# Layer 0 by dense scores and layers 1 to 3 with TensorE in program order, in place of layer 0 on neighbour lists

## The chip, the core and the metric

The kernel runs on one core of a Trainium2 chip. The time is the device time of one execution in microseconds, the median of several runs. The core's engines work side by side and wait for each other through semaphores: PE (TensorE, matrix products; PEld is its weight load), DVE (VectorE), ACT (ScalarE), POOL (GpSimd) and SP (SyncE, which only issues transfers). SBUF is the on-chip memory, PSUM the memory into which TensorE writes.

## The reference

Four graph attention layers over 3327 nodes with 256 features, all on one adjacency matrix `adj` (3327 x 3327, about 33 neighbours a node, itself included). After each layer comes x = layernorm(x + layer(x)). All is float32.

```python
# layer 0: additive scores, a leaky relu inside the sum over the 256 channels
g = leaky_relu(g_src[:, None, :] + g_tgt[None, :, :], 0.2)
score = where(adj != 0, einsum('ijc,c->ij', g, a_w), -inf)
x = layernorm(x + softmax(score) @ g_tgt)
# layer 1: e = leaky_relu(s1[:, None] + s2[None, :]); softmax over neighbours; @ Wh
# layer 2: the same without the leaky relu
# layer 3: two passes of a layer with four heads of 64 channels, each followed by elu
```

Layer 0 is the expensive one if it is done densely: its relu stands inside the channel sum, so a score needs 256 relus for each pair of nodes. Layers 1 to 3 have scores of the form relu(s_i + t_j), which are made from two vectors.

## The kernel before

Nodes lie in 26 row tiles of 128 (the last has 127), held as `h[0]` to `h[25]`.

**Layer 0 (`sparse0`).** Two projections of every tile are made (lines 228 and 233); the target rows go to a table in HBM. Then, tile by tile, `neighbours` (lines 244 to 297) makes a list of up to 56 neighbour numbers of each row on DVE from the adjacency, and casts the transposed adjacency to bf16 for the later layers (`turned` on ACT, line 277, stored to `at_d`). For each list place one gather on POOL's queue fetches 128 table rows (line 310); DVE makes the scores (lines 319 to 329), ACT the softmax weights (line 337), and each weight becomes a diagonal matrix on ACT (line 343) by which TensorE adds up the gathered rows (line 344). `lost` counts neighbours that found no place in a list. If there are any, a branch at the program's end runs `dense0` and `layers` over again; with these inputs it isn't taken.

**`dense0`** (lines 357 to 522) stands in the program for that branch. For a row tile it makes three passes over the columns (1024, 1024 and 1279 wide). A row's relu over all targets is one instruction on `[128 channels, width]`, the row's source value being a scalar for each channel; five of eight go to DVE, three to ACT (`turn % 8`). TensorE then sums over the channels with the attention vector: a 32-column window of zeros with the vector in one column puts the result into the row's own PSUM partition. Four rows, one in each group of 32 partitions, form a set that is multiplied span by span (512 wide). The relus have eight buffers, which is two sets. `finish0` makes softmax and the weighted sum in pieces that are dealt out among the next tile's sets.

**Layers 1 to 3 (`layers`).** Target columns are taken in four blocks of 7, 7, 6 and 6 tiles. Within a block a step is one tile j of 128 source nodes. `weigh` makes a step's weights for the block's columns: a relu on ACT (line 633), then plus one and times the adjacency on DVE (line 637), in a tile `e` that has six buffers. `one_head` (layers 1 and 2) multiplies them with the features into one PSUM bank for each tile of the block (line 730). `many_heads` (layer 3, run twice) makes eight products of 64 columns a step (line 769: four heads, two column halves, two heads sharing a bank), and eight sums of weights of 32 columns (line 776: four heads share a bank); the loop takes a half's four products and then its four sums. At a block's end come reciprocal, spread over the channels by a small product, and elu (lines 788 to 801). `pending` holds generators that prepare the next layer, taken on by one piece a step (`work_off`); `work_until` empties it where something is needed.

**Order.** The framework's scheduler orders the instructions of each engine ahead of time by priorities and expected times; the program order is only its starting point. In a layer-3 step it let the products of 64 columns alternate with the sums of 32.

Of the kernel before, what the change touches and what calls it, by code (L numbers as in the profile page):

```python
# [17 lines left out]
P = 128  # L18
# [5 lines left out]

KMAX = 56
CHUNK = 64
CHUNKS = 52
PIECES = 4

ROW = 260  # L30
# [3 lines left out]
def gat_stack(  # L34
# [55 lines left out]
    table_d = dram.tile([nt * P, ROW], F32, name="table_d")  # L90
# [30 lines left out]
    def attend(it, prob, proj, pool, psum, acc, col, width, copies):  # L121
# [45 lines left out]
    def residual_norm(dst, acc, total, skip, pn):  # L167

        inv = small.tile([P, 1], F32, tag="inv", name="inv")
        nc.vector.reciprocal(inv[:pn], total[:pn])  # L170
        y = work.tile([P, dim], F32, tag="y", name="y")
        nc.vector.scalar_tensor_tensor(
            y[:pn], acc, inv[:pn], skip, op0=ALU.mult, op1=ALU.add
        )
        norm(dst, y[:pn], pn)
# [7 lines left out]


    def sparse0(lost):
        with ExitStack() as s0:
            const0 = s0.enter_context(tc.tile_pool(name="s_const", bufs=1))
            io0 = s0.enter_context(tc.tile_pool(name="s_io", bufs=2))
            gath = s0.enter_context(tc.tile_pool(name="gath", bufs=11))
            ps0 = s0.enter_context(tc.tile_pool(name="s_ps", bufs=2, space=PSUM))  # L190

            w_src = const0.tile([P, kc, dim], F32, name="w_src0")
            nc.sync.dma_start(w_src, w_src_t.rearrange("(c p) f -> p c f", p=P))
            w_tgt = const0.tile([P, kc, dim + 1], F32, name="w_tgt0")
            nc.sync.dma_start(w_tgt[:, :, :dim], w_tgt_t.rearrange("(c p) f -> p c f", p=P))
            a_row = load_row(a_w, "src")
            bs_row = load_row(b_src, "dst")
            bt_row = load_row(b_tgt, "bias")
            dots(w_tgt[:, :, dim : dim + 1], w_tgt, a_row, 1)
            nc.vector.tensor_scalar_mul(  # L200
                w_tgt[:, :, dim], w_tgt[:, :, dim], SLOPE / (1.0 - SLOPE)
            )
            n_pad = CHUNK * CHUNKS
            rev = const0.tile([P, n_pad], F32, name="rev")
            for lo in range(0, n_pad, n_pad // PIECES):
                rev_i = io0.tile([P, n_pad // PIECES], I32, tag="adj_i", name="rev_i")
                nc.gpsimd.iota(
                    rev_i, pattern=[[-1, n_pad // PIECES]], base=n - lo, channel_multiplier=0
                )
                nc.vector.tensor_copy(rev[:, lo : lo + n_pad // PIECES], rev_i)  # L210

            x_t_p = x_t.rearrange("(c p) n -> p c n", p=P)
            for it in range(nt):
                pn = rows_of(it)
                xt = io0.tile([P, kc, P], F32, tag="xt", name="xt")
                nc.sync.dma_start(xt[:, :, :pn], x_t_p[:, :, it * P : it * P + pn])
                row = io0.tile([P, ROW], F32, tag="row", name="row")
                nc.vector.memset(row[:, dim + 1 :], 0.0)  # L220
                if pn < P:
                    nc.vector.memset(row[:, :dim], 0.0)
                    nc.vector.memset(row[:, dim : dim + 1], -BIG)
                    nc.vector.memset(h[it], 0.0)
                pt = ps0.tile([P, BANK], F32, tag="pt", name="pt")
                pss = ps0.tile([P, BANK], F32, tag="ps", name="pss")
                for k in range(kc):
                    nc.tensor.matmul(
                        pt[:pn, : dim + 1], xt[:, k, :pn], w_tgt[:, k, :],
                        start=(k == 0), stop=(k == kc - 1),  # L230
                    )
                for k in range(kc):
                    nc.tensor.matmul(
                        pss[:pn, :dim], xt[:, k, :pn], w_src[:, k, :],
                        start=(k == 0), stop=(k == kc - 1),
                    )
                nc.vector.tensor_add(row[:pn, :dim], pt[:pn, :dim], bt_row[:pn])
                nc.scalar.copy(row[:pn, dim : dim + 1], pt[:pn, dim : dim + 1])
                nc.vector.scalar_tensor_tensor(
                    h[it][:pn], pss[:pn, :dim], -1.0, bs_row[:pn],  # L240
                    op0=ALU.mult, op1=ALU.subtract,
                )
                nc.sync.dma_start(table_d[it * P : (it + 1) * P, :], row)

            def neighbours(it):

                pn = rows_of(it)
                cand = io0.tile([P, CHUNKS, 8], F32, tag="cand", name="cand")
                sums = io0.tile([P, PIECES + 1], F32, tag="sums", name="sums")
                per = CHUNKS // PIECES  # L250
                for s in range(PIECES):
                    lo = s * per * CHUNK
                    hi = min(n, lo + per * CHUNK)
                    adj_i = io0.tile([P, per * CHUNK], I32, tag="adj_i", name="adj_i")
                    nc.sync.dma_start(
                        adj_i[:pn, : hi - lo], adj[it * P : it * P + pn, lo:hi]
                    )
                    v = io0.tile([P, per * CHUNK], F32, tag="num", name="num")
                    if pn < P:
                        nc.vector.memset(v, 0.0)  # L260
                        nc.vector.memset(sums[:, s : s + 1], 0.0)
                    elif hi - lo < per * CHUNK:
                        nc.vector.memset(v[:, hi - lo :], 0.0)
                    nc.vector.scalar_tensor_tensor(
                        v[:pn, : hi - lo], adj_i[:pn, : hi - lo], 0.0, rev[:pn, lo:hi],
                        op0=ALU.not_equal, op1=ALU.mult, accum_out=sums[:pn, s : s + 1],
                    )
                    for c in range(per):
                        nc.vector.max(  # L269
                            cand[:, s * per + c, :], v[:, c * CHUNK : (c + 1) * CHUNK]  # L270
                        )
                    turned_i = io0.tile([P, per * CHUNK], I32, tag="turned_i", name="turned_i")
                    nc.sync.dma_start(
                        turned_i[:pn, : hi - lo], adj_t[it * P : it * P + pn, lo:hi]
                    )
                    turned = io0.tile([P, per * CHUNK], BF16, tag="turned", name="turned")
                    nc.scalar.copy(turned[:pn, : hi - lo], turned_i[:pn, : hi - lo])  # L277
                    nc.sync.dma_start(at_d[it * P : it * P + pn, lo:hi], turned[:pn, : hi - lo])
                found = io0.tile([P, KMAX], F32, tag="found", name="found")
                for r in range(0, KMAX, 8):  # L280
                    nc.vector.max(found[:, r : r + 8], cand)
                    if r + 8 < KMAX:
                        nc.vector.match_replace(
                            out=cand, in_to_replace=found[:, r : r + 8], in_values=cand,
                            imm_value=0.0,
                        )
                nc.vector.tensor_reduce(
                    sums[:, PIECES : PIECES + 1], found, axis=AX.X, op=ALU.add, negate=True
                )
                nc.vector.tensor_reduce(  # L290
                    lost[:, it : it + 1], sums, axis=AX.X, op=ALU.add
                )
                index = io0.tile([P, KMAX], mybir.dt.uint32, tag="index", name="index")
                nc.vector.tensor_scalar(
                    index, found, -1.0, float(n), op0=ALU.mult, op1=ALU.add
                )
                return index

            GROUP = 8
            for it in range(nt):  # L300
                pn = rows_of(it)
                index = neighbours(it)
                xr = io0.tile([P, dim], F32, tag="xr", name="xr")
                nc.sync.dma_start(xr[:pn], x[it * P : it * P + pn, :])
                sc = io0.tile([P, KMAX], F32, tag="scores", name="scores")
                gs = []
                for k0 in range(0, KMAX, GROUP):
                    g = gath.tile([P, GROUP, ROW], F32, tag="g", name="g")
# [214 lines left out]

# [433 lines left out]
```

## Time and profile before

| | |
|---|---|
| median of 3 runs | 5398.13 us (5394.32 to 5399.33) |
| the profiled execution | 5394.32 us, span 5392.5 us |
| mean granted TensorE clock | 0.801 |
| PE busy | 3236.2 us, 60% of the span |
| DVE busy | 2670.5 us, 50% |
| ACT busy | 1733.2 us, 32% |
| POOL busy | 1560.0 us, 29% |

The profile is of one execution. A group of instructions is named by line, engine, operation, output and inputs, with its number (x), its busy time in us, the mean duration of one in ns, and the idle time of the engine in front of them with what ended it. A float32 product leaves two records of TensorE. The stretches used below are cut where the last instruction of layer 0 ends (2829 us), where layer 2's products begin (3213), and at the begin and end of the two layer-3 passes (3545, 4461, 5364).

### The profile page before, as it was taken

To read this page: it belongs to the slowest core of one execution; us is meant where nothing else is said; L and a number is where in the kernel's file an instruction comes from. 1 tells how busy PE (TensorE), PEld (TensorE's weight loads), DVE (VectorE), ACT (ScalarE), POOL (GpSimd) and SP (SyncE) were. 2 spreads that over 40 slices of the span, in tenths; PEclk is the share of its full clock that TensorE was granted. 3 is DMA by queue.
4 is the path that set the end of the run, shared out by engine and by line. 5 is a ranking of instruction groups with operands and counts; after the bars stand their busy time and mean duration, and the time that the engine had idled before them with its cause. 6 is when DMAs were issued, how large, how long until landed. Compare 5 with 4: busy or idle time off the path is not lost.

```text
span 5392.5 us, 45944 instructions
## 1 busy us (share of the span) xinstructions
PE 3236.2 (60%) x14134; PEld 1624.5 (30%) x14134; DVE 2670.5 (50%) x7569; ACT 1733.2 (32%) x3049; POOL 1560.0 (29%) x1504
## 2 busy tenths in 40 slices
PE   4232121231231231232149999999999999999998
PEld 3131121221231131131137887642222222222222
DVE  6455255555555555555543541134445554455555
ACT  1243111221221121131133431134445554444544
POOL 2655266556556556556540000000000000000000
PEclk8666566666566676565669999999999999999999
DMA  8888344544545544544532222211000010010110
GB/s 254 180 215 209 68 98 93 87 95 93 88 94 93 88 94 94 84 97 94 83 62 57 63 63 75 59 40 28 21 25 23 25 29 23 26 30 27 31 31 23
DMA packets 199258, 413.05 MB, mean 77 GB/s; under 512 B 40830, under 2 KB 125800, under 8 KB 199008
## 3 DMA queue, kind: packets, MB, share of 16 engines
q0 software_dynamic: 69888, 193.92, 21.5%
q1 hardware_dynamic: 129120, 216.12, 13.8%
q8 instruction: 118, 1.93, 0.1%
q14 instruction: 132, 1.08, 0.1%
HBM read 380.89 MB, written 29.01 MB: 76 GB/s over the span
## 4 chain that ended last, share of the span: by engine, by line
PE 44%; DVE 2%; DMA 1%; POOL 1%; issue 1%; ACT 1%; POOLq 0%; SPq 0%; DVEq 0%; ACTq 0%
PE acc L769 17%; PE acc L776 13%; PE acc L730 8%; PE misc L617 2%; PE misc L578 2%; POOL g L310 1%; DMA at<-at_d 1%; PE acc L344 1%; PE misc L658 0%; DMA g<-table_d,index 0%; ACT e L633 0%; DVE stats L700 0%; DVE h L743 0%; POOL rstds L704 0%; DVE e L637 0%
## 5 line engine op out<-in xcount | busy, mean ns | idle before, releaser
L344 PE MATMUL acc<-g,diag 128*128 128x256 f32 x2912 | 697.2, 404 | 2039.3 <-ACT diag L343 2036.2
L310 POOL DMA_INDIRECT g<-table_d,index x1456 | 1520.8, 1044 | 1230.8 <-PE acc L344 708.6
L637 DVE SCALAR_TENSOR_TENSOR e<-e,at 128x896 f32<-128x896 f32 (+2 forms) x936 | 927.0, 1024 | 1012.5 <-ACT e L633 952.3
L633 ACT ACTIVATE e<-rate,minus_one,feat 128x896 f32<-128x896 f32 (+2 forms) x936 | 946.3, 1071 | 973.6 <-PE acc L776 849.5
L344 PEld LDWEIGHTS acc<-g,diag 128*128 128x128 f32 x2912 | 591.7, 205 | 2144.8 <-ACT diag L343 2056.3
L769 PE MATMUL acc<-e,feat 128*64 128x384 f32 (+4 forms) x3328 | 1007.2, 535 | 9.5 <-DVE e L637 9.2
L319 DVE TENSOR_TENSOR y<-g,h 128x1024 f32<-128x1024 f32 x364 | 444.6, 1223 | 926.4 <-DMA g<-table_d,index 926.4
L776 PE MATMUL acc<-e,feat 128*32 128x384 f32 (+4 forms) x3328 | 783.9, 525 | 0.0
L704 POOL TENSOR_TENSOR rstds<-rstds,minus_half 128x7 f32<-128x7 f32 (+1 forms) x12 | 20.1, 1676 | 2528.3 <-DVE rstds L703 2453.1
L343 ACT ACTIVATE diag<-ident,w 128x128 f32<-128x128 f32 x1456 | 544.4, 398 | 59.7 <-PE acc L344 29.7
L337 ACT ACTIVATE w<-scores,top 128x56 f32<-128x56 f32 x26 | 8.9, 341 | 1671.1 <-DVE top L334 1671.1
L325 DVE SCALAR_TENSOR_TENSOR y<-y,src 128x256 f32<-128x256 f32 x1456 | 525.7, 419 | 0.1
L769 PEld LDWEIGHTS acc<-e,feat 128*64 128x64 f32 (+1 forms) x3328 | 250.1, 135 | 712.9 <-issue 527.1
L730 PE MATMUL acc<-feat,e 128*128 128x257 f32 (+2 forms) x1352 | 306.7, 380 | 0.0
L776 PEld LDWEIGHTS acc<-e,feat 128*32 128x32 f32 (+1 forms) x3328 | 123.3, 107 | 577.9 <-issue 572.7
L730 PEld LDWEIGHTS acc<-feat,e 128*128 128x128 f32 (+2 forms) x1352 | 253.8, 190 | 35.7 <-issue 1.6
L730 PE MATMUL acc<-feat,at 128*128 128x257 bf16 (+2 forms) x2028 | 247.8, 279 | 16.0 <-DMA at<-at_d 16.0
L730 PEld LDWEIGHTS <-at 128*128 128x128 bf16 (+2 forms) x2028 | 202.7, 101 | 61.2 <-DMA at<-at_d 17.1
L277 ACT CAST turned<-turned_i 128x832 bf16<-128x832 int32 (+1 forms) x104 | 91.9, 883 | 395.9 <-DMA turned_i<-in_adj_t_dram 395.7
L269 DVE MAX8 cand<-num 128x8 f32<-128x64 f32 x1352 | 217.8, 212 | 1.8 <-DMA table_d<-row 1.4
L163 DVE TENSOR_SCALAR h<-y,mv,rstd 128x256 f32<-128x256 f32 (+1 forms) x26 | 12.0, 460 | 288.0 <-POOL rstd L162 288.0
L325 DVE DVE_READ_ACCUMULATOR y<-y,src 128x1 f32 x1456 | 118.8, 82 | 0.0
(108 smaller groups left out, 1490.5 us busy)
## 6 DMA issues: line engine op xcount, KB each, us to landing
at<-at_d SPq DMA_DIRECT2D x200, 224.0 KB
turned_i<-in_adj_t_dram SPq DMA_DIRECT2D x75, 416.0 KB
adj_i<-in_adj_dram SPq DMA_DIRECT2D x75, 416.0 KB
g<-table_d,index POOLq DMA_INDIRECT x1456, 3.6
at<-at_d SPq DMA_DIRECT2D x100, 192.0 KB
at<-at_d SPq DMA_DIRECT2D x100, 191.8 KB
at_d<-turned SPq DMA_DIRECT2D x75, 208.0 KB
adj_i<-in_adj_dram SPq DMA_DIRECT2D x25, 415.5 KB
```

Of the source, the lines that this page charges most:

```text
L269: nc.vector.max(cand[:, s * per + c, :], v[:, c * CHUNK : (c + 1) * CHUNK])
L310: nc.gpsimd.indirect_dma_start(out=g[:, s, :], out_offset=None, in_=table_d[:, :], in_offset=bass.IndirectOffsetOnAxis(ap=index[:, k0 + s ...
L319: nc.vector.tensor_tensor(y, g[:, part : part + 4, :dim], h[it][:, None, :].to_broadcast([P, 4, dim]), op=ALU.max,)
L325: nc.vector.scalar_tensor_tensor(y[:, s, :], y[:, s, :], 1.0, a_row, op0=ALU.mult, op1=ALU.mult, accum_out=sc[:, k : k + 1],)
L343: nc.scalar.activation(diag, ident, AF.Copy, scale=w[:, k : k + 1])
L344: nc.tensor.matmul(acc[:, :dim], diag, gs[k // GROUP][:, k % GROUP, :dim], start=(k == 0), stop=(k == KMAX - 1),)
L578: nc.tensor.matmul(pacc[:pn, : dim + nh], ht[:, k, :pn], self.weight[:, k, :], start=(k == 0), stop=(k == kc - 1),)
L633: nc.scalar.activation(e[:pn, : c1 - c0], self.rate[b][:pn, h_of, : c1 - c0], AF.Relu, bias=minus_one[:pn], scale=q,)
L637: nc.vector.scalar_tensor_tensor(e[:pn, : c1 - c0], e[:pn, : c1 - c0], 1.0, at[:pn, : c1 - c0], op0=ALU.add, op1=ALU.mult,)
L730: nc.tensor.matmul(accs[s][:pn, : dim + 1], a[:pj, s * P : s * P + pn], f[:pj, : dim + 1], start=(j == 0 and part == 0), stop=(j == nt - 1 ...
L769: nc.tensor.matmul(accs[x][p][q * hd : (q + 1) * hd, : hi - lo], f[:pj, h_of * hd : (h_of + 1) * hd], es[h_of][:pj, lo:hi], start=(j == 0) ...
L776: nc.tensor.matmul(accs[x][pairs][h_of * 32 : (h_of + 1) * 32, : hi - lo], f[:pj, dim + h_of : dim + h_of + 1].to_broadcast([pj, 32]), es[ ...
```

## The change

Layer 0 is done by the dense path alone: `sparse0`, its lists, the table, the branch and the second copy of the layers are gone, and what was `dense0` stands at the program's start. Two things are added to it: the transposed adjacency for the later layers is read, cast on POOL and stored to `at_d` in the tile loop. In layers 1 to 3, from the first block of layer 1 on, TensorE's instructions keep the program's order (the other engines are still scheduled); a step of layer 3 makes the products of both column halves and then the sums of both; preparing is split into finer pieces and begun from the fifth step of a block on; `e` has eight buffers in place of six, `at` three in place of four. The diff without changes of indentation, cut (the lines that are only moved are left out):

```diff
-    def sparse0(lost):
...
-    def dense0():
-        with ExitStack() as l0:
+    with ExitStack() as l0:
...
         for it in range(nt):
...
             z = io0.tile([P, n], F32, tag="z0", name="z0")
             for lo, hi in zip(cuts, cuts[1:]):
                 width = hi - lo
+                turned_i = io0.tile([P, widest], I32, tag="turned_i", name="turned_i", bufs=1)
+                nc.sync.dma_start(turned_i[:pn, :width], adj_t[it * P : it * P + pn, lo:hi])
+                turned = io0.tile([P, widest], BF16, tag="turned", name="turned", bufs=1)
+                nc.gpsimd.tensor_scalar(
+                    turned[:pn, :width], turned_i[:pn, :width], 0, 0,
+                    op0=ALU.is_equal, op1=ALU.is_equal,
+                )
+                nc.sync.dma_start(at_d[it * P : it * P + pn, lo:hi], turned[:pn, :width])
+            for lo, hi in zip(cuts, cuts[1:]):
...
-        edges = rs.enter_context(tc.tile_pool(name="edges", bufs=4))
+    edges = ctx.enter_context(tc.tile_pool(name="edges", bufs=3))
...
-                e = edges.tile([P, wide], F32, tag="e", name="e", bufs=6)
+            e = edges.tile([P, wide], F32, tag="e", name="e", bufs=8)
...
     def prepare(nxt, b, banks):
         for ht, it in turn(b, banks):
             at0 = (it - blocks[b][0]) * P
+            yield
             nxt.project(it, ht[:, :, at0 : at0 + P], banks)
             yield
...
+    LATER = 4
...
+                if j >= LATER:
                     work_off()
...
                 for x, (lo, hi) in enumerate(parts):
-                        for p in range(pairs):
-                            for q in range(2):
-                                h_of = 2 * p + q
+                    for h_of in range(layer.nh):
+                        p, q = divmod(h_of, 2)
                         nc.tensor.matmul(
                             accs[x][p][q * hd : (q + 1) * hd, : hi - lo],
...
+                for x, (lo, hi) in enumerate(parts):
                     for h_of in range(layer.nh):
                         nc.tensor.matmul(
                             accs[x][pairs][h_of * 32 : (h_of + 1) * 32, : hi - lo],
...
+    ctx.enter_context(tc.manual_schedule(engines={mybir.EngineType.PE}))
     one_head(l1, l2, (7,))
...
-    lost = nodes.tile([P, nt], F32, name="lost")
-    sparse0(lost)
-    with ExitStack() as rs:
-        layers(rs)
...
-    with tc.If(again > 0):
-        dense0()
-        with ExitStack() as rs:
-            layers(rs)
```

The core of the dense path, which was in the branch before and is now always run, with the lines of the changed kernel:

```python
                for q in range(G):                                    # G = 32
                    groups = [g for g in range(P // G) if g * G + q < pn]
                    for c in range(kc):                               # two halves of the channels
                        rs = []
                        for g in groups:
                            i = g * G + q
                            r = relus.tile([P, widest], F32, tag="relu", name="relu")
                            if turn % 8 in (1, 4, 6):
                                nc.scalar.activation(                 # line 321
                                    r[:, :width], tgt_t[:, c, lo:hi], AF.Relu,
                                    bias=src[:, c, i : i + 1],
                                )
                            else:
                                nc.vector.tensor_scalar(              # line 326
                                    r[:, :width], tgt_t[:, c, lo:hi],
                                    src[:, c, i : i + 1], 0.0, op0=ALU.add, op1=ALU.max,
                                )
                            turn += 1
                            rs.append(r)
                        for b0, b1 in spans:                          # 512 wide at most
                            for g, r in zip(groups, rs):
                                nc.tensor.matmul(                     # line 334
                                    sc[g * G : (g + 1) * G, b0:b1],
                                    window[:, c, G - 1 - q : 2 * G - 1 - q],
                                    r[:, b0:b1], start=False, stop=...,
                                )
                    next(pending, None)                               # a piece of finish0
```

## The prediction

> **What bounds the kernel now.** I read the table of stretches first, then the groups by form, then the time line of one layer-3 step. In the stretches the columns are length, busy time of PE, PEld, DVE, ACT and POOL (instructions), granted PE clock, DMA share, GB/s.
>
> ```profile
> 100.00:2829.00 2729.00, 697.18 (x2912) 591.66 (x2912) 1418.69 (x5617) 630.37 (x1598) 1532.29 (x1479) 0.63 0.54 108
> 2829.00:3213.00 384.00, 369.33 (x1663) 305.02 (x1664) 175.33 (x343) 158.10 (x290) 5.60 (x4) 0.97 0.23 62
> 3213.00:3545.00 332.00, 310.78 (x2280) 241.21 (x2277) 56.10 (x185) 41.50 (x120) 5.59 (x4) 0.97 0.26 68
> 3545.00:4461.00 916.00, 910.41 (x3597) 232.08 (x3596) 459.37 (x512) 448.13 (x527) 2.03 (x1) 1.00 0.09 25
> 4461.00:5364.00 903.00, 884.23 (x3456) 208.06 (x3456) 474.42 (x561) 434.09 (x466) 6.13 (x3) 0.99 0.10 27
> ```
>
> Layer 0 on lists takes 2829 us, 109 us a row tile, paced by the 1456 gathers on POOL and what waits for them; no engine is full and TensorE is at 0.63 of its clock. Layers 1 and 2 (384 and 332 us) and the two layer-3 passes (916 and 903 us) are TensorE throughout, at full clock; there DVE and ACT are half idle. Then the time line of TensorE in layer 3 (start, length, group):
>
> ```profile
> 4000.69 1.72 PE L769 MATMUL acc<-e,feat 128*64 128x384 f32 x4
> 4002.33 1.05 PE L776 MATMUL acc<-e,feat 128*32 128x512 f32 x2
> 4003.31 1.07 PE L769 MATMUL acc<-e,feat 128*64 128x512 f32 x2
> 4004.31 1.04 PE L776 MATMUL acc<-e,feat 128*32 128x512 f32 x2
> 4005.29 1.51 PE L769 MATMUL acc<-e,feat 128*64 128x384 f32 x6
> 4006.72 0.85 PE L776 MATMUL acc<-e,feat 128*32 128x384 f32 x8
> 4007.50 1.08 PE L769 MATMUL acc<-e,feat 128*64 128x512 f32 x4
> 4008.51 1.05 PE L776 MATMUL acc<-e,feat 128*32 128x512 f32 x4
> ```
>
> A float32 product leaves two records. One 512-wide product of 32 columns holds TensorE 0.98 us (4002.33 to 4003.31), and four of them at 384 together only 0.78 (4006.72 to 4007.50): products on different column groups run at once, if they stand together. The next step begins at 4009.49, so a step costs 8.81 us, eight changes between 64 and 32 columns in it. A lone 512 group streams 4x512 columns, 0.86 us at 2.4 columns a ns, and 0.12 to 0.13 is left for the change.
>
> **What the Trainium skill says.** "TensorEngine Tiling (Array Packing)", Key Properties: tiles operate independently, and a change of tiling mode drains TensorE; both agree with the lines above. "VectorE: DVE Perf Modes", the perf-mode tier table: a float32 `tensor_scalar` from SBUF runs at 2x. "ScalarE: Activation LUTs", What ACT_TABLE_LOAD costs: 0.833 ns an element, about 93 ns for each pointer operand, and 93 ns overlap back to back. The trace agrees with these two:
>
> ```profile
> L799 DVE TENSOR_SCALAR spread_s<-o 128x384 f32<-128x384 f32 x20 | 6.5, 352 | 0.0
> L799 DVE TENSOR_SCALAR spread_s<-o 128x512 f32<-128x512 f32 x8 | 3.0, 420 | 0.0
> L601 DVE TENSOR_SCALAR v<-v 128x256 f32<-128x256 f32 x25 | 8.8, 352 | 5.1 <-ACT v L600 5.1
> L800 ACT ACTIVATE spread_s<-spread_s 128x384 f32<-128x384 f32 x20 | 9.7, 515 | 9.9 <-DVE spread_s L799 9.9
> L800 ACT ACTIVATE spread_s<-spread_s 128x512 f32<-128x512 f32 x8 | 4.6, 622 | 4.8 <-DVE spread_s L799 4.8
> ```
>
> DVE: 68 ns for 128 elements, 0.53 each, so 148 + 0.53 N; at 256 a pointer scalar costs 352 - 284 = 68 more. ACT: 0.836 each, 194 + 0.836 N without a pointer. Back to back, DVE operations (L325, L709) start 83 ns before the end of the one in front, ACT's (L633) 95 ns.
>
> **Part 1, layer 0.** Removed: all up to 2829 us, and the guard at the end (the last 10 us). Added, always run: the dense score. For each of 26 row tiles, three passes of 1024, 1024 and 1279 columns, each with 256 relu operations (160 DVE, 96 ACT) and 64 sets of four 32-column products.
> - TensorE. A 512 span of four column groups is one stream, 0.86 us; a 255 span 0.43. Sets: 64 x (1.72 + 1.72 + 2.15) = 357.8. The full-width score terms (28 products: 24 of 0.86, 4 of 0.43) 22.4; pgs 0.9; 26 transposes of 0.21 (L658) 5.5; 26 weighted sums of 0.46 (L730 float32, 289/625) 12.0; some 34 mode changes of 0.13, 4.4. Sum 403 us a tile.
> - DVE. Relu at 1024: 148 + 533 + 68 = 749, every 666 ns; at 1279: 882, every 799. 160 x (0.666 x 2 + 0.799) = 341, plus masks, score writes, one reduction of 3327, copies and norm, some 16 (estimate at one cycle an element, from L319's 1.2 us at 1024): 357.
> - ACT. Relu at 1024: 194 + 92 + 853 = 1139, every 1044; at 1279 every 1257. 96 x 3.345 = 321, plus exp and copies 6: 327.
>
> So TensorE is the bound, at a load that kept the clock at 1.00 in layer 3. Above 403: eight relu buffers are two sets, and a set's last relu is followed by its two or three spans before its buffer is free. Where the column groups run on their own, the first three groups of a set free theirs a span earlier, and 5 DVE relus of 0.666 (3.33 us) fit under two sets (3.44); a wait of 30 ns on each (as L637 starts 30 ns after L633 ends) makes that 3.48, so some 5 us a tile. Once a tile ACT's exp stands behind the score write (1.5), five relus (3.4), the reduction (3.6): some 5. Copies queued on DVE and ACT behind TensorE's transposes, with relus behind them: some 5. I take 418.5; 26 tiles: 10,880. Before it some 60: 7 chunks of 4 x 0.86 + 8 x 0.43 on TensorE are 48, and the first product starts at 10. After it the last tile's softmax, transposes and sum with nothing to cover them: 40.
>
> The transposed adjacency goes to POOL (78 casts). The trace has no such cast; the nearest, its IOTA of 832 (820 ns), gives 1.1 us, 85 us in all; the skill's "GPSIMD Engine Reference", Specifications, says POOL contends with DVE in a 2-port mode, so up to all 85 could hold DVE. No row here shows it; since TensorE has a margin, I take 40, ends 0 and 150 (at 1.9 us each). Its loads and stores queue on SP in front of adjacency loads, which are due only every 140 us; hidden.
>
> **Part 2, layers 1 and 2.** Same products, PE in program order. They are at 96% PE (369 of 384, 311 of 332), so order can't win much; the transposes and projections of the next layer, now begun from the fifth step on, keep off a just-finished block. 717 stays, ends -25 and +40.
>
> **Part 3, layer 3.** A step's eight products (two column halves) together, then its eight sums: two mode changes for eight. Blocks of seven tiles: a 64-column group streams two at 512 and two at 384, 3.01; sums 0.86 + 0.65; changes 0.26: 4.77 for 8.81. ACT needs 4 x 1.025 = 4.1 and DVE 4.0, so it stays TensorE. Eight weight tiles are two steps: the next-but-one step's last weight is ready 5.3 us after its buffers come free, needed at 4.77 + 0.86. Blocks of six: 2.58 + 1.29 + 0.26 = 4.13; there the same chain gives 4.76 against 4.78, so take 4.2. A pass: 52 x 4.8 + 52 x 4.2 = 468. Between blocks, in program order, TensorE stands for reciprocal and elu (3.4, 2.5, then the row of L797 to L801, some 12), then projections and rates (18): 26 in the first pass, 15 in the second: 163 for all. Layer 3: 2 x 468 + 163 = 1099 for 1819. Norm and stores at the end 15.
>
> **Sum** against the profiled execution (5394.3 us, span 5392.5; the median of the runs, 5398.1, is 0.07% above): 60 + 10,880 + 40 + 40 + 717 + 1099 + 15 = 12,851. I say 12,850. A change within 0.2%, about 11 us, could not be told from none.
>
> **Rivals.**
> - A set acts as one unit: its buffers come free only when all its products end. Then ACT's two relus of a set (2.18), two waits, the set (1.72) and its 0.17 us of drain follow one another: 4.15 us for two sets at 1024, 5.0 at 1279, with TensorE 80% busy. A tile: 32 x 13.3 + 22 + 15 = 463, the total 14,000. For it: eight buffers are few. Against: at 4735 us in the trace a 384 and a 512 product on two column groups each go on to their second half when their own first half ends.
> - Layer 3 gives little, because program order exposes what the scheduler hid between blocks (20 us a block now) or the weights come late: layer 3 at 1500, the total 13,250.
> - TensorE never waits in layer 0: 403 x 26, no POOL loss: 12,400.
> - The column groups don't overlap here: 4 x 358 a tile, above 40,000. The x8 row speaks against it.
> - Not slower: the dense score runs within 5398 - 1931 = 3467 us, 133 us a tile, 2.1 us for two sets at 1024. Since nothing but the relus and the products is left, it would need float32 products in one pass instead of four (90 us) and relus at 0.27 us each on both engines; L799's 0.53 ns an element excludes it. Nor does the time before contain the dense path: no instruction of lines 357 to 522 is in its trace.
>
> **Chances.** Forecast (12,600 to 13,100) 0.50, one unit or half-way to it 0.23, layer 3 poor 0.09, no waits 0.13, groups serial or another large loss 0.045, not slower 0.005. The range 12,300 to 14,100 leaves out the last two and the outer ends.
>
> **What would show it.** PE busy above 92% in layer 0 at clock 1.00, the relu on DVE near 750 ns and on ACT near 1140, relu buffers waiting for TensorE, not the other way. If L334 instead waits for DVE or ACT for a fifth of the time, the one-unit rival holds. Layer 3: 4.8 us a step, two groups in it. Wrong would be a relu on DVE at 1.28 us (1x; one every 1.20, at 1279 1.47): DVE then sets 160 x 3.87 + 16 = 635 us a tile; or a clock under 0.95.

## The result, and the profile after

| | before | after |
|---|---|---|
| median of 4 runs | 5397.07 us (5394.32 to 5399.33) | 13,173.4 us (13,172.4 to 13,179.0) |
| ratio | | 2.441, 95% interval 2.437 to 2.445 |
| span of the profiled execution | 5392.5 us | 13,171.1 us |
| mean granted TensorE clock | 0.801 | 0.985 |
| PE busy | 60% of the span | 96% |

The forecast was 12,850 us. The table of stretches of the kernel after (length, then busy time of PE, PEld, DVE, ACT and POOL, granted PE clock, DMA share, GB/s) is cut at the first relu (57), at the last score write of the second row tile (1140), at the end of the last tile's scores (11,203), of layer 0 (11,238), of layers 1 and 2 (11,618, 11,955), at the first product of layer 3 (12,008) and at its last sum (13,140):

```profile
57.00:1140.00 1083.00, 873.93 (x7375) 356.62 (x7374) 849.84 (x983) 674.15 (x585) 315.95 (x74) 0.92 0.20 62
1140.00:11203.00 10063.00, 9919.13 (x89393) 4101.52 (x89392) 8731.44 (x11949) 8094.01 (x7078) 23.46 (x24) 1.00 0.02 6
11203.00:11238.00 35.00, 21.63 (x82) 16.02 (x82) 8.92 (x16) 5.28 (x6) 0.07 (x1) 0.76 0.06 20
11238.00:11618.00 380.00, 368.34 (x1660) 307.96 (x1660) 176.84 (x342) 158.60 (x289) 5.51 (x4) 0.96 0.23 62
11618.00:11955.00 337.00, 301.50 (x2279) 241.83 (x2277) 56.25 (x191) 43.55 (x122) 5.59 (x4) 0.95 0.25 67
11955.00:12008.00 53.00, 33.63 (x72) 15.97 (x74) 14.46 (x34) 7.58 (x26) 2.03 (x1) 0.61 0.05 13
12008.00:13140.00 1132.00, 1077.78 (x6982) 416.77 (x6978) 916.45 (x1033) 873.03 (x964) 4.27 (x3) 0.97 0.16 41
```

The long second line is the dense score: 24 row tiles in 10,063 us, 419.3 each, TensorE 99% busy at full clock, DVE 87% and ACT 80%. The first two tiles, in which nearly all of POOL's casts run, take 1083. Layer 3 fell from 1819 us to 1132, and a new stretch of 53 us stands before it. The groups by form of the kernel after (busy time, mean ns of one, idle time before and what ended it) show that the operations cost what was worked out from layer 3:

```profile
L334 PE MATMUL sc<-relu,window 128*32 128x512 f32 x79848 | 9764.6, 595 | 350.9 <-DVE relu L326 201.6 <-ACT relu L321 149.3
L326 DVE TENSOR_SCALAR relu<-tgt_t,src 128x1024 f32<-128x1024 f32 x8318 | 5774.6, 761 | 645.0 <-PE sc L334 606.9 <-ACT src L276 0.4
L321 ACT ACTIVATE relu<-tgt_t,src 128x1024 f32<-128x1024 f32 x4990 | 5424.8, 1142 | 1257.5 <-PE sc L334 1253.4
L326 DVE TENSOR_SCALAR relu<-tgt_t,src 128x1279 f32<-128x1279 f32 x4158 | 3492.7, 892 | 611.3 <-PE sc L334 522.6
L321 ACT ACTIVATE relu<-tgt_t,src 128x1279 f32<-128x1279 f32 x2496 | 3225.3, 1353 | 944.3 <-PE sc L334 944.3
```

A relu is expected at 749, 1139 and 882 ns and takes 761, 1142 and 892; both engines' waits are mostly for `PE sc L334`, for a buffer that TensorE has not yet given back. (How much time that costs TensorE itself, the 99% don't tell; see run 4.) The time line of TensorE in layer 3 after (start, length, group) answers to the one shown of before:

```profile
12059.97 3.23 PE L600 MATMUL acc<-e,feat 128*64 128x512 f32 x16
12063.12 1.71 PE L608 MATMUL acc<-e,feat 128*32 128x512 f32 x16
12064.76 3.23 PE L600 MATMUL acc<-e,feat 128*64 128x512 f32 x16
```

A step is 12,064.76 - 12,059.97 = 4.79 us with two groups in it, where it was 8.81 with eight changes.

Forecast and trace, part by part:

| part | forecast | measured |
|---|---|---|
| before the first relu | 60 | 57 |
| 26 row tiles and POOL's casts | 10,880 + 40 | 1083 + 10,063 = 11,146 |
| last tile's softmax and sum | 40 | 35 |
| layers 1 and 2 | 717 | 380 + 337 = 717 |
| between layers 2 and 3 | not in the sum | 53 |
| layer 3 | 1099 | 1132 |
| end | 15 | 31 |
| sum | 12,851 | 13,171 |

Of the 320 us that are missing, 226 are in the row tiles: 24 tiles at 419.3 for 418.5 make 19, the first two at 1083 for 837 make 246, and 40 of these 265 were set aside for the casts, which run in the first two tiles. The trace after shows how. The instructions of the tile `turned` on POOL (minimum, median and maximum ns, first and last start):

```profile
L285 POOL TENSOR_SCALAR turned<-turned_i x78: 3625/4262/5706, 17.9 to 798.5; 128x1024 bf16<-128x1024 int32 x50, 128x1279 bf16<-128x1279 int32 x25, 127x1024 bf16<-127x1024 int32 x2, 127x1279 bf16<-127x1279 int32 x1
```

The same view of the norm's `rstd` up to 1300 us:

```profile
L154 DVE TENSOR_SCALAR rstd<-mv x2: 153/154/155, 652.0 to 1224.1; 128x1 f32<-128x1 f32 x2
L155 POOL TENSOR_TENSOR rstd<-rstd,minus_half x2: 574/808/1042, 803.0 to 1224.3; 128x1 f32<-128x1 f32 x2
```

The longest wait of DVE between 600 and 830 us (total us, times, longest):

```profile
DVE h L156 <- POOL rstd L155: 150.8, 1, 150.8
```

The last of POOL's instructions before that norm goes on (in square brackets, what POOL waited for before each):

```profile
719.42 3.64 POOL L285 TENSOR_SCALAR turned<-turned_i 127x1024 bf16<-127x1024 int32 x1 [23.83 <-DMA turned_i<-in_adj_t_dram]
756.59 3.62 POOL L285 TENSOR_SCALAR turned<-turned_i 127x1024 bf16<-127x1024 int32 x1 [33.53 <-DMA turned_i<-in_adj_t_dram]
798.51 4.54 POOL L285 TENSOR_SCALAR turned<-turned_i 127x1279 bf16<-127x1279 int32 x1 [38.30 <-DMA turned_i<-in_adj_t_dram]
803.02 0.57 POOL L155 TENSOR_TENSOR rstd<-rstd,minus_half 128x1 f32<-128x1 f32 x1
```

The relu of line 326 from 57 to 653 us, and from 1140 us on, in the view of one line's instructions:

```profile
L326 DVE TENSOR_SCALAR relu<-tgt_t,src x561: 729/744/5230, 57.2 to 652.1; 128x1024 f32<-128x1024 f32 x134, 128x1279 f32<-128x1279 f32 x53
L326 DVE TENSOR_SCALAR relu<-tgt_t,src x11516: 731/751/892, 1140.9 to 11196.8; 128x1024 f32<-128x1024 f32 x132, 128x1279 f32<-128x1279 f32 x67
```

A cast takes 3.6 us or more, not 1.1. Only their own two tiles, of one buffer each, hold the casts back, so all 78 run in the first 803 us. Tile 0's norm is ready at 652.0 on DVE, but its power stands on POOL's queue behind the casts of all later tiles and starts at 803.0. DVE, in order, waits 150.8 us with the relus of tile 1 behind it. POOL itself is mostly idle in that time: eight casts take 32 us, and their waits for their loads 119. The three loads of the last row tile, which has 127 rows, make up 96 of these. Each kept POOL waiting for 24 to 38 us, where the loads of 128 rows just before left 4.3 to 5.2; while POOL waited for the last, from 762 to 798 us, the DMA share was 0.06, one of 16 engines. The trace of before has the same: its four casts of 127 rows, then on ACT, waited 25 to 32 us for their loads.

The second loss is in the relus. Before 653 us most are unchanged (median 744 ns), but single ones last up to 5.2 us; in later tiles none is over 0.89. Counted from the trace, about 100 of the 561 are lengthened, by 138 us together, each of them within 0.2 us of a cast: some 78 by at most 0.9 us, the others by 1.5 to 4.3.

### The profile page after: what moved, and what is told of

It reads as the page before. It is cut to its first block, busy times and chain, and to the rows that moved or that the text cites. A ratio compares the mean times of both kernels' runs of the same rounds, so it can differ in the third digit from the quotient of the medians.

```text
span 13171.1 us, 262064 instructions
## 1 busy us (share of the span) xinstructions
PE 12653.4 (96%) x108020; PEld 5491.9 (42%) x108020; DVE 10785.2 (82%) x14619; ACT 9870.7 (75%) x9093; POOL 378.4 (3%) x122
## 4 chain that ended last, share of the span: by engine, by line
PE 77%; ACT 10%; issue 6%; DMA 4%; POOL 3%; DVE 1%; SPq 0%; POOLq 0%; DVEq 0%; ACTq 0%
PE sc L334 56%; ACT relu L321 10%; PE acc L600 5%; PE acc L561 4%; DMA turned_i<-in_adj_t_dram 3%; POOL turned L285 3%; PE acc L138 2%; PE acc L608 2%; PE sc L304 2%; PE sc L309 2%; PE misc L444 1%; PE misc L405 1%; PE ptp L123 1%; DMA at<-at_d 0%; DVE invs L621 0%
## 5 line engine op out<-in xcount | busy, mean ns | idle before, releaser
L321 ACT ACTIVATE relu<-tgt_t,src 128x1024 f32<-128x1024 f32 (+1 forms) x7486 | 8647.8, 1212 | 2201.8 <-PE sc L334 2197.7
L326 DVE TENSOR_SCALAR relu<-tgt_t,src 128x1024 f32<-128x1024 f32 (+1 forms) x12476 | 9265.2, 805 | 1256.3 <-PE sc L334 1129.5
L334 PE MATMUL sc<-relu,window 128*32 128x512 f32 (+1 forms) x93156 | 9789.9, 564 | 350.9 <-DVE relu L326 201.6
L334 PEld LDWEIGHTS sc<-relu,window 128*32 128x32 f32 x93156 | 3867.1, 109 | 6026.9 <-issue 2599.5
L464 DVE SCALAR_TENSOR_TENSOR e<-e,at 128x896 f32<-128x896 f32 (+2 forms) x936 | 923.0, 1024 | 345.7 <-ACT e L460 280.6
L600 PE MATMUL acc<-e,feat 128*64 128x384 f32 (+4 forms) x3328 | 647.7, 524 | 0.1
L138 PE MATMUL acc<-proj,pt 128*128 128x256 f32 (+2 forms) x1352 | 344.2, 396 | 4.9 <-DVE pt L132 2.9
L285 POOL TENSOR_SCALAR turned<-turned_i 128x1024 bf16<-128x1024 int32 (+2 forms) x78 | 334.9, 4293 | 466.9 <-DMA turned_i<-in_adj_t_dram 466.9
L304 PE MATMUL sc<-tgt_t,qa_wide 128*128 128x512 f32 (+1 forms) x728 | 334.0, 570 | 0.0
L608 PE MATMUL acc<-e,feat 128*32 128x384 f32 (+4 forms) x3328 | 333.4, 519 | 0.0
L309 PE MATMUL sc<-qa_wide,src 128*128 128x512 f32 (+1 forms) x728 | 319.5, 561 | 0.0
```

The source lines that it names most:

```text
L138: nc.tensor.matmul(acc, pt[:w, j - j0, :pn], proj[:w, j, col : col + width], start=(j == 0), stop=(j == nt - 1),)
L285: nc.gpsimd.tensor_scalar(turned[:pn, :width], turned_i[:pn, :width], 0, 0, op0=ALU.is_equal, op1=ALU.is_equal,)
L304: nc.tensor.matmul(sc[:, b0:b1], qa_wide[:, c, :P], tgt_t[:, c, lo + b0 : lo + b1], start=(c == 0), stop=False, skip_group_check=True,)
L309: nc.tensor.matmul(sc[:, b0:b1], src[:, c, :], qa_wide[:, c, : b1 - b0], start=False, stop=False, skip_group_check=True,)
L321: nc.scalar.activation(r[:, :width], tgt_t[:, c, lo:hi], AF.Relu, bias=src[:, c, i : i + 1],)
L326: nc.vector.tensor_scalar(r[:, :width], tgt_t[:, c, lo:hi], src[:, c, i : i + 1], 0.0, op0=ALU.add, op1=ALU.max,)
```

## The experiments

Beside the experiments the kernel before took 5463 us (the first four), 5520 (the next four) and 5370 (the last two), for 5397 above; so stretches within a trace are compared, and the dense tiles, 419.3 us in every run that didn't touch them, show that these agree. Runs 1 to 8 are one execution each, so a difference of a few us between their totals says nothing.

**1. The casts on ACT.**

```diff
-                nc.gpsimd.tensor_scalar(
-                    turned[:pn, :width], turned_i[:pn, :width], 0, 0,
-                    op0=ALU.is_equal, op1=ALU.is_equal,
-                )
+                nc.scalar.copy(turned[:pn, :width], turned_i[:pn, :width])
```

> The changed kernel with the 78 casts of the transposed adjacency on ACT in place of POOL. Theory A (the casts hold DVE instructions[...], 138 us of lengthened relus before 650 us, and the norm's power waits behind them on POOL, 151 us): both go, the first tile takes 395 to 405 us instead of 502, the second 420 instead of 581, total 12,890 to 12,930. ACT's 78 casts of about 1.1 us fit into its idle quarter. Rival B (only the wait of the power behind the casts costs; the first tile is slow for another reason, a cold clock or the loads): first tile stays near 500, total 13,010 to 13,030.

Measured 13,013.3 us. That total is rival B's, and the tiles are not: the second tile ends 154 us earlier, at 986 us for 1140, the norm waits 0.5 us, and the longest relu is 0.89 us. So both losses of theory A were POOL's casts, but its gain was too large by about 100 us: the second tile ends 102 us later than in the next run, for a reason that neither theory had. The waits of ACT in this run from 57 to 1100 us (total us, times, longest):

```profile
ACT relu L318 <- PE sc L331: 115.4, 154, 9.3
ACT turned L285 <- DMA turned_i<-in_adj_t_dram: 96.8, 20, 31.3
```

ACT is in order too: a cast that waits for its load holds the relus behind it, 97 us, of which 79 are the same three loads of the last row tile. TensorE waits 82 us for ACT's relus in these two tiles.

**2. The casts on POOL, but no further ahead than the adjacency loads** (`turned_i` takes turns with `adj_i` in two buffers).

```diff
-                turned_i = io0.tile([P, widest], I32, tag="turned_i", name="turned_i", bufs=1)
+                turned_i = io0.tile([P, widest], I32, tag="adj", name="turned_i")
```

> The changed kernel with the casts still on POOL, but their input tile shares the two buffers of the adjacency tile, so that each row tile makes its own three casts (all casts ran ahead in the first 800 us before). Theory A: the 151 us wait of the norm goes; DVE is still held by each cast, some 1.8 us on average, 5 us a tile, of which its slack takes part: total 12,900 to 13,040, first tile 400 to 425. Rival B (only crowding hurts, nothing is lost when the casts are spread): 12,900 and tiles of 419.3. Rival C (the shared buffers put adjacency loads late): tiles above 425.

Measured 12,993.8 us. The stretch of the first two tiles in the kernel with paced casts, against 1083 us:

```profile
57.00:883.80 826.80, 814.28 (x7413) 345.24 (x7412) 726.38 (x989) 671.37 (x589) 18.85 (x6) 1.00 0.04 11
```

PE is busy 814 of 827 us, so the 256 us of loss in these tiles are gone. The lengthened relus are not: 71 of them, 120 us in all, now lie over the whole run, and the later tiles take about 421.4 instead of 419.3. Nor is the queue harmless now. POOL meets the loads of the last row tile in the second to last, and there the norm's power, ready at 10,238.4, stands behind them again:

```profile
10264.72 4.54 POOL L285 TENSOR_SCALAR turned<-turned_i 127x1279 bf16<-127x1279 int32 x1 [38.30 <-DMA turned_i<-in_adj_t_dram]
10269.23 0.57 POOL L155 TENSOR_TENSOR rstd<-rstd,minus_half 128x1 f32<-128x1 f32 x1
```

DVE waits 30.7 us for it, and this one tile takes 451.6. So of the 256 us some 77 are lost again later, and 180 are gained in all, within theory A's range. What cost most was thus the run ahead (a queue of casts that wait for loads, and 78 casts within two tiles), not the casts' work.

**3. Layers 1 to 3 left to the scheduler**, all else as in the changed kernel.

```diff
-    ctx.enter_context(tc.manual_schedule(engines={mybir.EngineType.PE}))
```

> The changed kernel without program order on TensorE: the scheduler orders all engines again. Theory A (the order of the step's groups gives layer 3 its gain): layer 3 back from 1132 to about 1800 us, total 13,800 to 13,860. Rival B (the loops as written and eight weight tiles give it, whatever the scheduler does): total 13,130 to 13,250.

Measured 13,152.1 us, 21 less than the changed kernel. Layer 3 takes 1172 us from first product to last sum, with 4.80 us a step, and begins at 11,946, without the gap. Program order for TensorE is not what brought layer 3 down.

**4. Ten relu buffers** on top of the paced casts.

```diff
-        relus = l0.enter_context(tc.tile_pool(name="relus", bufs=8))
+        relus = l0.enter_context(tc.tile_pool(name="relus", bufs=10))
```

> The casts paced as in the run before, and ten relu buffers in place of eight. Theory A (in the 1279-wide pass TensorE waits because two sets of buffers don't cover relu, wait and drain; its own work is 8.9 + 32 x 4.30 = 146.5 us of the 159.4): third pass 147 to 152, 1024-wide passes unchanged at 117.0, tile 408 to 413, total 12,600 to 12,850. Rival B (the 255-wide spans cost TensorE more than their stream, or DVE paces): third pass stays above 157, total as with paced casts alone.

Measured 12,562.7 us, 404.5 a tile, better than theory A's range. Stretches of a second and a third pass of row tile 10, first of the changed kernel, then with ten buffers:

```profile
4636.50:4753.60 117.10, 117.10 (x1039) 54.60 (x1040) 111.40 (x163) 103.78 (x97) 0.00 (x0) 1.00 0.02 6
4753.60:4912.90 159.30, 153.34 (x1561) 56.48 (x1561) 132.15 (x159) 121.80 (x95) 0.00 (x0) 1.00 0.02 6
```

```profile
4228.90:4346.60 117.70, 117.70 (x1042) 40.74 (x1043) 111.27 (x163) 103.50 (x97) 0.00 (x0) 1.00 0.02 6
4346.60:4492.30 145.70, 145.70 (x1560) 53.97 (x1559) 128.79 (x160) 120.98 (x94) 0.00 (x0) 1.00 0.02 6
```

With eight buffers the 1024-wide pass already runs at TensorE's own pace; only the 1279-wide one waits, 13.6 us a tile, and two more buffers take all of it. Of these 13.6 us only 6 show as idle time of PE with eight buffers (159.30 less 153.34); the rest is within its busy time, and so an engine that was 99% busy had 14.8 us a tile to give. Against the paced kernel the gain is 16.9 us a tile, since the first pass, in which the casts lie, falls too, from 145.1 to 141.3. The stall behind the last row tile's loads stays: one tile takes 439.7 us. Why two sets of buffers are enough for two spans and not for three was not tried.

**5 and 6. Which part of the layer-3 change works: tiles or loop.** Run 3 has the new loop and eight weight tiles, before has the old loop and six; these two are the other corners, all four ordered by the scheduler. (The rest of before differs from the other three; run 9 below, which is before with the new loop and eight tiles, takes 1168 us where run 3 takes 1172, so the difference doesn't matter.) Run 5 puts the old loop back:

```diff
                 for x, (lo, hi) in enumerate(parts):
                     for h_of in range(layer.nh):
...
-                for x, (lo, hi) in enumerate(parts):
                     for h_of in range(layer.nh):
                         nc.tensor.matmul(
                             accs[x][pairs][h_of * 32 : (h_of + 1) * 32, : hi - lo],
```

> The changed kernel with layers 1 to 3 left to the scheduler and with the layer-3 loop of before (for each column half its four products, then its four sums), but with eight weight tiles. The order it is built with has some 4.3 changes between 64- and 32-column groups in a step; before had about 8 with six weight tiles, the run with the new loop 2.2 with eight. Theory A (what costs is that a half's products of different heads do not stand together; six tiles forced them apart, since only two heads of the next step can be ready): the groups fill here, so a step of seven row tiles costs 1.72 + 0.86 + 1.29 + 0.65 + 4 x 0.13 = 5.05 us, layer 3 some 1172 + 208 x 0.26 = 1,226 us (1,200 to 1,260). Rival C (the new loop is what matters): near the 1,817 us of before, 8.8 us a step. Rest of the kernel as in the run without program order.

Run 6 keeps the new loop:

```diff
-            e = edges.tile([P, wide], F32, tag="e", name="e", bufs=8)
+            e = edges.tile([P, wide], F32, tag="e", name="e", bufs=6)
```

> The changed kernel with layers 1 to 3 left to the scheduler and with the new layer-3 loop, but with six weight tiles as before. It is built with some 4 changes a step. Theory B (the tiles limit): the tiles of heads 2 and 3 of a step come free only when the sums of the step before them have ended, so each step waits for two activations and a product of its own, some 3 us; 7.5 us a step on average, layer 3 some 1,700 to 1,800 us. Theory A (the order alone): 5.05 us a step and 1,200 to 1,260 us. Rival C (the new loop is what matters): the same 1,172 to 1,260. So B is told from A and C here, and A from C by the run with the old loop and eight tiles.

| layer 3, first product to last sum | six weight tiles | eight |
|---|---|---|
| old loop | 1818 us (before) | 1242 us (run 5) |
| new loop | 1406 us (run 6) | 1172 us (run 3) |

TensorE's time line in a block of seven, old loop with eight tiles, then new loop with six:

```profile
12059.93 1.94 PE L600 MATMUL acc<-e,feat 128*64 128x512 f32 x8
12061.80 1.06 PE L607 MATMUL acc<-e,feat 128*32 128x512 f32 x8
12062.79 1.51 PE L600 MATMUL acc<-e,feat 128*64 128x384 f32 x8
12064.23 0.85 PE L607 MATMUL acc<-e,feat 128*32 128x384 f32 x8
12065.01 1.94 PE L600 MATMUL acc<-e,feat 128*64 128x512 f32 x8
```

```profile
12061.18 1.93 PE L600 MATMUL acc<-e,feat 128*64 128x512 f32 x8
12063.04 1.70 PE L608 MATMUL acc<-e,feat 128*32 128x512 f32 x14
12064.67 1.72 PE L600 MATMUL acc<-e,feat 128*64 128x512 f32 x8
12066.32 1.04 PE L608 MATMUL acc<-e,feat 128*32 128x512 f32 x2
12067.30 1.93 PE L600 MATMUL acc<-e,feat 128*64 128x512 f32 x8
```

With eight tiles the old loop's groups fill: 5.08 us a step for the 5.05 expected, and 1242 us are within theory A's range. With six, the new loop doesn't wait as theory B had it (1700 to 1800 us); TensorE is busy 1368 of 1406 us. The order the scheduler chose starts with two heads' products and draws sums in between, and the last record of sums shows the price: one 512-wide sum alone (x2, from 12,066.32) holds TensorE 0.98 us, when four together take 0.99 (12,061.80 to 12,062.79). A step is 6.12 us. So theory C falls in both runs, and run 6 lies between A and B: too few tiles cost, not as a wait but as groups that don't fill. Eight tiles alone bring 576 of the 646 us, the loop alone 412. What the new loop with six tiles does in program order was not run.

**7. The old loop in program order**, eight tiles; the same diff as run 5, on the changed kernel.

> The changed kernel whole, TensorE in program order and eight weight tiles, with only the layer-3 loop put back (a half's products, then its sums: exactly 4 changes a step instead of 2). If a change costs 0.13 us, as read from the trace of before: 4.80 + 0.26 = 5.06 us a step at seven row tiles, layer 3 1,132 + 208 x 0.26 = 1,186 us. If the change costs nothing where groups follow on directly: 1,132. If the old loop itself is what was slow: above 1,500.

Layer 3 takes 1165.8 us against 1132.8, 33.0 more in place of the expected 54. A step in a block of seven:

```profile
12060.70 1.94 PE L600 MATMUL acc<-e,feat 128*64 128x512 f32 x8
...
12065.79 1.94 PE L600 MATMUL acc<-e,feat 128*64 128x512 f32 x8
```

It takes 5.09 us against 4.79 to 4.80 in the changed kernel, so two more changes cost 0.29 here, 0.145 each, somewhat more than the 0.13 that was read from the trace of before. Over all eight blocks the steps take 999 us for 953, 47 more for 416 changes, 0.11 each; but between the blocks 166 us pass for 180, which hides 14 of it. Why that is was not looked into. With filled groups even the written-out old order is within 3% of the new one.

**8. No draining before a block.**

```diff
-            work_until(lambda: layer.rate[b] is not None and not pending)
+            work_until(lambda: layer.rate[b] is not None)
```

> The changed kernel with one condition taken away: a layer-3 block waits at its start only for its own rates, no longer until all work of the block before has been issued; that work goes between the steps from the fifth on. Theory A (in program order TensorE stands in that work for ACT and DVE): the 53 us at the start of layer 3 shrink to some 12, and each of the four blocks of the first pass loses 5 to 15 us of its 31 to 35 us before the next: 40 to 100 us less in all, layers 1 to 3 at 1,820 +- 30 us for 1,902. Rival: the time there is TensorE's own work (33.6 of the 53 us it is busy) and only moves: 0 to 25 us less. A second rival: the waits move along with it into the steps, since program order makes TensorE wait wherever the work stands: no gain or a loss.

Measured 13,146.2 us, 27 less than the changed kernel; layers 1 to 3 end at 13,114 instead of 13,140 from the same 11,238. That is the rival, barely above its 25. What stands in the gap of the changed kernel is shown by TensorE's time line there, layer 2 ending in the first row:

```profile
11950.03 4.06 PE L561 MATMUL acc<-feat,at 127*128 127x257 bf16 x18 [6.35 <-DMA at<-at_d]
11962.66 0.66 PE L485 MATMUL misc<-ident,h 128*128 128x128 f32 x2 [8.57 <-DVE h L540]
11963.84 2.10 PE L405 MATMUL misc<-l3aw,ht 128*128 128x260 f32 x4 [0.52 <-ACT ht L488]
11966.72 0.69 PE L485 MATMUL misc<-ident,h 128*128 128x128 f32 x2 [0.79 <-DVE feat L416]
...
11986.92 3.78 PE L444 MATMUL misc<-ht,w_src 128*128 128x512 f32 x4 [0.79 <-DVE feat L416]
...
11999.20 1.98 PE L444 MATMUL misc<-ht,w_src 128*128 128x512 f32 x4 [0.47 <-ACT rate L450]
```

First it waits 8.6 us for the norm, then for DVE and ACT by turns at each tile of the block, all through the one bank that this work has. The granted clock in the 53 us was 0.61, and the same products of L444 took 3.78 us at first and 1.98 later. With the work moved between the steps, from the end of layer 2 to the last sum TensorE's idle time falls from 73.6 to 57.0 us, and its busy time from 1111 to 1101.

**9 and 10. The layer-3 part on the kernel before.** Run 9 is the kernel before with the new loop and, cut to the two main lines,

```diff
-        edges = rs.enter_context(tc.tile_pool(name="edges", bufs=4))
+        edges = rs.enter_context(tc.tile_pool(name="edges", bufs=3))
...
-                e = edges.tile([P, wide], F32, tag="e", name="e", bufs=6)
+                e = edges.tile([P, wide], F32, tag="e", name="e", bufs=8)
```

The room comes also from `invs` with one buffer, `y` in the place of `spread`, and five buffers for the small tiles in place of six.

> The kernel before (layer 0 on neighbour lists, layers left to the scheduler) with only the layer-3 part of the change: the new loop and eight weight tiles (the room for them from one invs tile instead of two, three adjacency tiles instead of four, and y in the place of spread). If layer 3 is worth here what it is worth in the changed kernel, its 1,819 us become 1,172 as in the run without program order: 5,397 - 645 = 4,750 us, ratio 0.88 (4,720 to 4,790). Rival: the third adjacency tile or layer 0's end takes some of it back: above 4,850.

Run 10 adds program order, the finer pieces and later start of the preparing, and run 8's line.

> As the run before it, with TensorE in program order from layer 1 on, the other steps from the fifth step, and without the condition that a block waits for all work of the one before. In the changed kernel program order with that condition cost 21 us against the scheduler and taking the condition away brought 27 back: 4,745 us, 0 to 20 us below the run before it. Rival: without the dense layer 0 ahead of it the order matters more in layers 1 and 2 (before: 369 busy of 384 us and 311 of 332): 4,700 us.

Measured, medians of four executions: run 9 4734.8 us, ratio 0.8817 to before (0.8802 to 0.8831); run 10 4711.5 us, ratio 0.8774 (0.8759 to 0.8789). Both beat both kernels. The stretches of layer 3 in run 9 and in run 10, against 1819 us:

```profile
3532.00:4701.00 1169.00, 1136.79 (x7058) 421.22 (x7055) 929.76 (x1073) 879.65 (x990) 8.16 (x4) 0.99 0.15 41
```

```profile
3526.00:4683.00 1157.00, 1100.30 (x7053) 404.21 (x7052) 926.65 (x1069) 873.81 (x990) 8.15 (x4) 0.97 0.15 41
```

The gain of run 9 is layer 3's, 650 us; the rival with a loss at the adjacency tile falls. Run 10 is 23 us below it, slightly more than expected and half-way to its rival; in the traces layer 3 gives 12 of it and layers 1 and 2 give 11 (717 us for 728).

## Why the prediction was right

The change is slower by the factor that the dense score sets, and the pure work of the forecast's two large terms, the row tiles and layer 3's steps, was right by its own working. The total was right in part by luck: two terms were short by some 210 and 53 us, and the wide range took them in.

- **A row tile, 418.5 us: right, 419.3.** TensorE bounds it, at clock 1.00 in the 24 later tiles and with the relu durations worked out from layer-3 rows. (The sum for DVE's relu takes 533 ns for 1024 elements, 0.52 each, where the lines give 0.53 and so 543; the median of the trace, 749, is that of the sum.) With ten buffers a tile takes 404.5, so the 403 of pure work held. Two 1024-wide sets take 3.43 us, which is (117.0 - 7.1)/32, the pass's length less its eight full-width products, for 3.44 of pure TensorE time. But the 15.5 us of losses were put in the wrong place: the 5 us for 30 ns at each buffer in the 1024-wide passes did not occur, and run 4 puts 13.6 us into the 1279-wide pass alone. That the sum agrees is luck.
- **The one-unit rival fell only for two spans.** At 1024 two sets took 3.43 us, not its 4.15. At 1279 they took (159.4 - 8.9)/32 = 4.70, between the 4.30 of pure work and its 5.0. The prediction didn't work out this pass for its own case.
- **POOL's casts, 40 us with ends 0 and 150: wrong, some 250.** This is the term that failed. It was priced from the nearest row, an IOTA of 820 ns that reads nothing, and the upper end took 1.9 us a cast; the cast takes 3.6 and more. And only contention with DVE was asked about. The larger loss, 151 us in one wait, is another: a norm's power stands on the same in-order queue behind casts of later tiles, and these wait for their loads far longer (119 us) than they work (32). The loads were called hidden, since the adjacency tiles behind them on SP's queue are due late; what waits for them on POOL was not asked. Runs 1 and 2 each take the 151 us away, and both show what the slow loads of the last row tile still cost.
- **Layers 1 and 2, 717: missed by 53.** Their products take 380 + 337 us. But the forecast's stretch ends where layer 3's products begin, and to there it is 770, above its upper end of 757: the drain at a block's start leaves TensorE alone with transposes and rates. Left to the scheduler (run 3), the same stretch takes 708. That order can't win much there held; that it could lose was priced at 40 at most.
- **A layer-3 step, 4.77 and 4.2 us: right, 4.79 and 4.20** in steady state; with their first steps the blocks take 953 us for 936. Between the blocks it was 180 us for 163, though the last elu isn't among these 180 but in the end: the elu and its spread take about 14 and the projections and rates 20 in the first pass. The prediction's own parts, 12 and 18, make 30, and not the 26 that its sum took.
- **The rival "layer 3 gives little, because program order exposes what the scheduler hid"** had this mechanism, but priced it at 400 us; 53 came in front of layer 3 and 17 between the blocks.
- **The reason given for layer 3's gain** was the loop's order; the eight tiles were taken as enough for it. Runs 5 and 6 show them as the larger part.

The other rivals fell: the columns' groups did overlap; TensorE's waits were not nothing (12,400). The median lies inside the range, but 73 us above the likeliest case's own 13,100, among totals that were set aside for the one-unit rival and a poor layer 3, neither of which made it; with the casts sized at 250 instead of 40 the same sum gives 13,061.

## What to carry to other kernels

When work moves to a queue, ask who else uses that queue in order, how far the work can run ahead, and what it waits for itself: an instruction that waits for its load blocks the queue without being busy. A buffer shared with something that keeps pace took away 256 us of loss in two tiles here, but not the stall at the last row tile's slow loads. Where products on parts of the array can run together, count how many operands are ready at once: too few buffers show up as groups that don't fill on an engine that looks full, and busy time alone doesn't tell. The same holds for the relu buffers: TensorE was 99% busy, and two more buffers gave 15 us a tile. And before a bundle is judged by its total, run its parts: this one lost 7776 us as a whole, with an 11.8% gain inside it.

## What the runs showed of the hardware that was not expected

- An int32 to bf16 cast with two compares on POOL takes 3.63 us for 1024 elements a partition and 4.54 for 1279 at its fastest: (4543 - 3625)/255 = 3.6 ns an element, as the profile gives POOL's spans.
- While casts run on POOL, most DVE relus keep their duration (median 744 ns), but single ones lasted up to 5.2 us: the loss comes in a few large steps, not as an even slowdown. With the casts on ACT (run 1) no relu is over 0.89 us.
- Loads of the last row tile, 127 rows, kept their cast waiting for 24 to 38 us where loads of 128 rows just before left 4.3 to 5.2; the DMA share meanwhile was 0.06, one of 16 engines.
- A float32 product on one group of 32 columns holds TensorE as long as four on four groups: 0.98 and 0.99 us at 512.
- A change between 64- and 32-column groups costs TensorE 0.11 to 0.145 us also where filled groups follow on directly (run 7); the trace of before gave 0.12 to 0.13 where a group stands alone.
